# FFN weights rounded by quarters of the inner channels, part of them during block 0's FFN, with a shorter rounding and a two-operation norm end

## The chip, the core and the metric

The kernel runs on one core of a Trainium2 chip. The metric is the device time of one execution in microseconds. A core has engines that each work through a queue of their own in order: TensorE (PE in the profile; its weight loads are PEld), VectorE (DVE), ScalarE (ACT) and GpSimd (POOL). SyncE (SP) issues most of the DMAs. An instruction whose operands aren't ready holds up everything queued behind it on its engine. SBUF is the working memory of 128 partitions; PSUM holds what TensorE accumulates.

## The reference, cut to what matters

The input x has 4096 tokens (4 sequences of 1024) of 512 channels. Two residual parts follow each other; both begin and end with a layer norm (LN, without gain here unless named):

```
n   = LN(x)
q, v, g = n Wq^T, n Wv^T, silu(n Wg^T)
ret = scan over the tokens of a sequence: state = lambda * state + v
o   = ( LN(q * ret) * gamma + beta ) * g            # "attention's norm end"
x1  = x + LN(o Wo^T)

m    = LN(x1)
gate = silu( (m @ fp8(gate_w)) * gate_scale )       # 512 -> 1536 inner channels
up   =       (m @ fp8(up_w))   * up_scale
out  = x1 + LN( ((gate * up) @ fp8(down_w)) * down_scale )   # 1536 -> 512
```

`fp8(w)` rounds a float32 weight to float8 e4m3 and back to float32: three bits behind the leading one, a fixed step below 2^-6, and NaN for what is too large (the largest value is 448). It has to be done once for the three FFN matrices, 3 x 786,432 numbers, before they are used.

## The kernel before, in words

**Tiles and blocks.** The tokens are worked off in 8 blocks (`NB`) of 512 (`TB`), each in 4 groups (`NS`) of 128 tokens. Channels lie in `NC` = 4 chunks of 128, inner channels in `NI` = 12 chunks of 128.

**Attention** of a block is the generator `retention(t)` with `A_STEPS` = 17 steps. It norms and transposes x into `xnT`, projects (`project`, L191) onto v and q per chunk, scans (L228) and multiplies (L237) into `y`; takes the mean over channels with a matmul (`mu`, L241), subtracts it (L243), takes the variance the same way (L248 and L249) and forms `rstd` (L251 on ACT, L252 on DVE). Then per chunk c it projects onto g (L191, silu in L259) and finishes the norm on GpSimd: `y *= rstd` (L260), `y = y * gamma + lnb` (L261), `y *= g` (L265). Last, for each token group s, a matmul with Wo (L277), a norm of the result `o` (bn_stats L154 and L155, 1/sqrt on GpSimd in L159 and L160, scaling in L164), the residual sum on GpSimd (L284), a second norm giving `x1n`, and a transpose (L183) whose result is split into two float32r parts, `hi` by ACT (L184) and `lo` by DVE (L185), in the tile `x1nT`.

**FFN** of a block is `ffn(t)` with 13 steps. Step i projects onto gate and up for inner chunk i (`project_split`, L200, 8 matmuls each, since hi and lo both count), applies silu (L311), multiplies (L312), splits into `fuse` hi and lo (L314 on ACT, L315 on DVE), and issues the down projection of chunk i-1 (L301). The last step scales, norms, adds and stores the four groups (L323 to L326).

**Rounding** is the generator `round_weights()`: 12 pieces of 128 x 1536 numbers. Each piece gets a scratch tile `scr` (w and c side by side), a DMA of the weights into w (L136 or L138), and then seven DVE operations and one ACT operation (L139 to L148). Pieces 0 to 7 are rows of gate and up in turn (a chunk of 128 input channels, all 1536 inner ones), pieces 8 to 11 are down. So no inner chunk of gate is complete before the seventh piece.

**Buffers that count here.** `scr` and `x1nT` share the tag `"x1n"` of the pool `big`, which has two buffers: a piece that is being rounded takes one, and so does each block's `x1nT` from attention's Wo stage until the last matmul of that block's FFN. The pool `ps_a` of PSUM has two buffers (tag `"pa"`), used for all of attention's matmul results and transposes; `ps_f` has two for gate and up.

**Order.** The Python code emits work in an interleaved order, and the framework then lays out each engine's queue: work that was emitted earlier goes first, and an operation emitted later fills in where the earlier one isn't ready by the framework's own plan. At run time the queues are fixed. `together(main, main_steps, other, other_steps, after)` emits one step of `main`, then as many of `other` as keep it in proportion. Attention 0 is emitted with all 12 pieces; then FFN t with attention t+1; the last FFN alone. Tiles are tracked by region: the first down matmul of block 0 runs before the last piece of `down_sb` is written (174.98 us and 185.87 us in the trace).

Of the kernel before, what the change touches and what calls it, by code (L numbers as in the profile page):

```python
# [10 lines left out]
F32 = mybir.dt.float32  # L11
I32 = mybir.dt.int32
F32R = mybir.dt.float32r
AF = mybir.ActivationFunctionType
ALU = mybir.AluOpType

P = 128
# [5 lines left out]
def retention_ffn_sandwich(  # L23
# [19 lines left out]
    nc = tc.nc  # L43
    NT, D = x.shape
    I = gate_w.shape[1]
    NC = D // P
    NI = I // P
# [4 lines left out]
    const = ctx.enter_context(tc.tile_pool(name="const", bufs=1))  # L52
# [20 lines left out]
    def load_const(src, cols, name):  # L73
        t = const.tile([P, cols], F32, tag=name, name=name)
        nc.scalar.dma_start(t, src)
        return t
# [12 lines left out]
    gamma_sb = load_const(gamma, NC, "gamma_sb")  # L89
    lnb_sb = load_const(lnb, NC, "lnb_sb")  # L90
# [4 lines left out]
    gate_sb = wpool.tile([P, NC, I], F32R, tag="gate_sb", name="gate_sb")  # L95
    up_sb = wpool.tile([P, NC, I], F32R, tag="up_sb", name="up_sb")
    down_sb = wpool.tile([P, NI, D], F32R, tag="down_sb", name="down_sb")
    gate_v = gate_w.rearrange("(c p) f -> p c f", p=P)
    up_v = up_w.rearrange("(c p) f -> p c f", p=P)
    down_v = down_w.rearrange("(c p) f -> p c f", p=P)  # L100
    RC = NI // NC
    pieces = []
    for c in range(NC):
        pieces += [(gate_sb[:, c, :], gate_v[:, c, :]), (up_sb[:, c, :], up_v[:, c, :])]
    for c in range(NC):
        pieces.append((down_sb[:, RC * c : RC * c + RC, :], down_v[:, RC * c : RC * c + RC, :]))
    gs_sb = load_const(gate_s, NI, "gs_sb")
    us_sb = load_const(up_s, NI, "us_sb")
    ds_sb = load_const(down_s.to_broadcast([P, D]), D, "ds_sb")
# [5 lines left out]
    nc.vector.memset(mean_w, 1.0 / D)  # L115
    eps_sb = const.tile([P, 1], F32, tag="eps_sb", name="eps_sb")
    nc.vector.memset(eps_sb, EPS)
    nhalf = const.tile([P, NS], F32, tag="nhalf", name="nhalf")
    nc.vector.memset(nhalf, -0.5)
    carry = const.tile([P, NC], F32, tag="carry", name="carry")  # L120
# [7 lines left out]
    def round_weights():  # L128


        for n, (dst, src) in enumerate(pieces):
            scr = big.tile([P, 2, I], F32, tag="x1n", name=f"scr_{n}", bufs=2)
            w, c = scr[:, 0, :], scr[:, 1, :]
            if len(dst.shape) == 3:
                dst = dst.rearrange("p c f -> p (c f)")
                nc.sync.dma_start(w.rearrange("p (c f) -> p c f", f=D), src)  # L136
            else:
                nc.sync.dma_start(w, src)  # L138
            nc.vector.tensor_scalar(  # L139
                c.bitcast(I32), w.bitcast(I32), 0x7F800000, None, ALU.bitwise_and  # L140
            )
            nc.vector.tensor_scalar(c, c, 2.0**-6, 1.5 * 2.0**20, ALU.max, ALU.mult)
            nc.vector.tensor_tensor(w, w, c, ALU.add)
            nc.vector.tensor_tensor(w, w, c, ALU.subtract)
            nc.scalar.activation(c, w, AF.Square)
            nc.vector.tensor_scalar(c, c, 448.0**2, 448.0**2, ALU.max, ALU.subtract)
            nc.vector.tensor_scalar(c, c, 3.0e38, 0.0, ALU.mult, ALU.mult)
            nc.vector.tensor_tensor(dst, w, c, ALU.add)  # L148
            yield


    def stats(src, mv):
        st = small.tile([P, 6], F32, tag="st", name="st")
        nc.vector.bn_stats(st, src)  # L154
        nc.vector.bn_aggr(mv, st)  # L155
# [7 lines left out]
    def center_scale(dst, src, mean, rstd):  # L163
        nc.vector.tensor_scalar(dst, src, mean, rstd, ALU.subtract, ALU.mult)  # L164
# [41 lines left out]
    def retention(t, give):  # L206
        xt = xs[t]

        mv4 = small.tile([P, NS, 2], F32, tag="mv4", name="mv4")
        for s in range(NS):  # L210
            stats(xt[s], mv4[:, s, :])
        rstd4 = rstd_of(mv4[:, :, 1], NS)
        xnT = big.tile([P, NC, TB], F32, tag="xnT", name=f"xnT_{t}")
        for s in range(NS):
            xn = work.tile([P, D], F32, tag="tok", name=f"xn_{t}_{s}", bufs=5)
            center_scale(xn, xt[s], mv4[:, s, 0:1], rstd4[:, s : s + 1])
            to_channels(xnT, xn, s)
            if s % 2 == 1:
                yield


        y = big.tile([P, NC, TB], F32, tag="y", name=f"y_{t}")
        for c in range(NC):
            pv = project(ps_a, "pa", wv_sb, c, xnT)
            pq = project(ps_a, "pa", wq_sb, c, xnT)
            ret = work.tile([P, TB], F32, tag="ret", name=f"ret_{t}_{c}")
            first = (t * TB) % seq == 0
            nc.vector.tensor_tensor_scan(  # L228
                ret,
                lam[:, c : c + 1].to_broadcast([P, TB]),  # L230
                pv,
                0.0 if first else carry[:, c : c + 1],
                ALU.mult,
                ALU.add,
            )
            nc.vector.tensor_copy(carry[:, c : c + 1], ret[:, TB - 1 : TB])
            nc.vector.tensor_tensor(y[:, c, :], pq, ret, ALU.mult)  # L237
            yield
        mu = ps_a.tile([P, TB], F32, tag="pa", name=f"mu_{t}")
        for c in range(NC):  # L240
            nc.tensor.matmul(mu, mean_w, y[:, c, :], start=(c == 0), stop=(c == NC - 1))  # L241
        for c in range(NC):
            nc.vector.tensor_tensor(y[:, c, :], y[:, c, :], mu, ALU.subtract)  # L243
        yield
        var = ps_a.tile([P, TB], F32, tag="pa", name=f"var_{t}")
        for c in range(NC):
            sq = work.tile([P, TB], F32, tag="ret", name=f"sq_{t}_{c}")
            nc.scalar.activation(sq, y[:, c, :], AF.Square)  # L248
            nc.tensor.matmul(var, mean_w, sq, start=(c == 0), stop=(c == NC - 1))  # L249
        rstd = work.tile([P, TB], F32, tag="rstd", name=f"rstd_{t}", bufs=1)  # L250
        nc.scalar.activation(rstd, var, AF.Sqrt, bias=eps_sb)  # L251
        nc.vector.reciprocal(rstd, rstd)  # L252
        yield


        for c in range(NC):
            pg = project(ps_a, "pa", wg_sb, c, xnT)
            g = work.tile([P, TB], F32, tag="sg", name=f"g_{t}_{c}", bufs=3)
            nc.scalar.activation(g, pg, AF.Silu)  # L259
            nc.gpsimd.tensor_tensor(y[:, c, :], y[:, c, :], rstd, ALU.mult)  # L260
            nc.gpsimd.tensor_scalar(  # L261
                y[:, c, :], y[:, c, :], gamma_sb[:, c : c + 1], lnb_sb[:, c : c + 1],
                ALU.mult, ALU.add,
            )
            nc.gpsimd.tensor_tensor(y[:, c, :], y[:, c, :], g, ALU.mult)  # L265
            yield

        x1nT = big.tile([P, 2, NC, TB], F32R, tag="x1n", name=f"x1nT_{t}", bufs=2)  # L270
        hi, lo = x1nT[:, 0, :, :], x1nT[:, 1, :, :]
        give((hi, lo))
        before = None
        for s in range(NS):
            po = ps_a.tile([P, D], F32, tag="pa", name=f"po_{t}_{s}")
            for c in range(NC):
                nc.tensor.matmul(  # L277
                    po, y[:, c, ts(s, P)], wo_sb[:, c, :], start=(c == 0), stop=(c == NC - 1)
                )
            if before is not None:  # L280
                to_channels_split(hi, lo, before, s - 1)
            o = work.tile([P, D], F32, tag="tok", name=f"o_{t}_{s}", bufs=5)
            norm(o, po)
            nc.gpsimd.tensor_tensor(xt[s], xt[s], o, ALU.add)  # L284
            before = work.tile([P, D], F32, tag="tok", name=f"x1n_{t}_{s}", bufs=5)
            norm(before, xt[s])
            yield
        to_channels_split(hi, lo, before, NS - 1)
        yield
# [42 lines left out]
    A_STEPS = 2 + NC + 1 + 1 + NC + NS + 1  # L332
    given = {}

    def together(main, main_steps, other, other_steps, after=0):

        done = 0
        for k in range(main_steps):
            next(main)
            upto = -(-other_steps * (k + 1 - after) // (main_steps - 1 - after))  # L340
            while done < min(upto, other_steps):
                next(other)
                done += 1

    def start(t):
        return retention(t, lambda z: given.__setitem__(t, z))

    for s in range(NS):
        load_x(1, s)
    together(start(0), A_STEPS, round_weights(), len(pieces))  # L350
    for t in range(NB):
        if t + 1 < NB:
            together(ffn(t, given[t]), NI + 1, start(t + 1), A_STEPS, after=1)
        else:
            together(ffn(t, given[t]), NI + 1, None, 0)


# [42 lines left out]
```

## Time and profile before

The time is 1233.34 us (median of 3 runs, 1232.6 to 1235.83). The profiled execution has a span of 1229.2 us and a mean granted TensorE clock of 0.963.

| engine | busy us | share of the span |
|---|---|---|
| PE | 1087.4 | 88% |
| PEld | 678.0 | 55% |
| DVE | 569.6 | 46% |
| POOL | 294.0 | 24% |
| ACT | 245.2 | 20% |

| event in the trace | us from the span's start |
|---|---|
| first matmul of the projections (L191) | 16.00 |
| first rounding operation (L139) | 27.75 |
| end of the matmuls of `mu` (L241) | 52.30 |
| end of the reciprocal (L252) | 75.87 |
| end of the last norm-end operation on POOL (L265) | 98.56 |
| first gate matmul of FFN 0 (L200) | 166.14 |
| last rounding operation (L148) | 187.63 |
| first gate matmul of FFN 1 | 301.94 |
| first gate matmul of FFN 7 | 1144.98 |
| last matmul | 1213.29 |

From FFN 0 to FFN 7 there are seven periods in 978.8 us, that is 139.8 us each; the first of them is 135.8 us. A line of the page's groups reads: source line, engine, operation, output<-inputs, shapes, count, then busy time in us and the mean of one in ns, then the idle time of the engine just before these operations and who ended it.

### The profile page before, as it was taken

How to read it: one execution, taken by the hardware profiler on the slowest of the kernel's cores; microseconds unless marked ns; L12 is line 12 of the kernel's file. 1: busy time of each engine (PE TensorE's matmuls, PEld its weight loads, DVE VectorE, ACT ScalarE, POOL GpSimd, SP SyncE). 2: the span in 40 equal slices, each digit the busy share in tenths (PEclk: the TensorE clock that was granted, in tenths of full speed). 3: DMA queues.
4: the chain of work that ended last, by engine and by line, in shares of the span. 5: the costliest groups of instructions: out<-in, count | busy, mean ns of one | idle time of the engine just before them, and what ended most of it. 6: DMA issues, size and time to landing. Idle time of an engine off the chain costs nothing. (4 is left out here: it accounts for less than half of the span.)

```text
span 1229.2 us, 9606 instructions
## 1 busy us (share of the span) xinstructions
PE 1087.4 (88%) x3712; PEld 678.0 (55%) x3712; DVE 569.6 (46%) x865; ACT 245.2 (20%) x358; POOL 294.0 (24%) x374
## 2 busy tenths in 40 slices
PE   6673369999899979999899989999899989999994
PEld 3221155566466655665556655666556655665683
DVE  3986883326432473316523373315623363324523
ACT  1130130311113111311103111211203111131221
POOL 0054310233203240043303240043303241033302
PEclk9876689999999999999999999999999999999998
DMA  7120200000200020000200010000200000000000
GB/s 274 51 77 26 77 26 1 1 1 1 69 1 0 1 69 1 1 1 1 69 1 1 0 55 14 1 1 1 69 1 1 1 34 26 1 1 0 35 1 34
DMA packets 15054, 31.31 MB, mean 25 GB/s; under 512 B 2080, under 2 KB 2080, under 8 KB 15008
## 3 DMA queue, kind: packets, MB, share of 16 engines
q1 hardware_dynamic: 14144, 30.41, 7.2%
q8 instruction: 29, 0.48, 0.2%
q10 hardware_dynamic: 864, 0.28, 0.1%
q14 instruction: 17, 0.14, 0.0%
HBM read 22.30 MB, written 8.39 MB: 25 GB/s over the span
## 5 line engine op out<-in xcount | busy, mean ns | idle before, releaser
L200 PE MATMUL po_pf<-x1nT,gate_sb 128*128 128x512 f32 x768 | 218.4, 423 | 0.7 <-ACT x1nT L184 0.7
L200 PE MATMUL po_pf<-x1nT,up_sb 128*128 128x512 f32 x768 | 195.9, 393 | 11.9 <-DVE gate L312 11.9
L301 PE MATMUL pd<-down_sb,fuse 128*128 128x512 f32 x768 | 195.5, 394 | 10.0 <-DVE fuse L315 10.0
L200 PEld LDWEIGHTS po_pf<-x1nT,gate_sb 128*128 128x128 f32 x768 | 143.6, 189 | 56.1 <-issue 23.4
L312 DVE SCALAR_TENSOR_TENSOR gate<-po_pf,us_sb,gate 128x512 f32<-128x512 f32 x96 | 71.1, 740 | 213.8 <-PE po_pf L200 213.1
L301 PEld LDWEIGHTS pd<-down_sb,fuse 128*128 128x128 f32 x768 | 142.3, 188 | 46.1 <-DVE fuse L315 16.3
L200 PEld LDWEIGHTS po_pf<-x1nT,up_sb 128*128 128x128 f32 x768 | 143.6, 188 | 43.5 <-DVE gate L312 14.8
L260 POOL TENSOR_TENSOR y<-y,rstd 128x512 f32<-128x512 f32 x32 | 46.1, 1460 | 497.8 <-DVE rstd L252 497.8
L277 PE MATMUL po<-wo_sb,y 128*128 128x512 f32 x256 | 123.1, 626 | 17.8 <-POOL y L265 9.6
L311 ACT ACTIVATE gate<-po_pf,gs_sb 128x512 f32<-128x512 f32 x96 | 66.2, 689 | 303.7 <-PE po_pf L200 271.0
L191 PE MATMUL po_pa<-xnT,wq_sb 128*128 128x512 f32 x256 | 116.9, 600 | 2.1 <-DVE y L237 2.1
L191 PE MATMUL po_pa<-xnT,wv_sb 128*128 128x512 f32 x256 | 115.2, 593 | 1.5 <-DVE ret L228 0.8
L191 PE MATMUL po_pa<-xnT,wg_sb 128*128 128x512 f32 x256 | 114.5, 595 | 0.0
L314 ACT CAST fuse<-gate 128x512 fp32r<-128x512 f32 x96 | 59.9, 624 | 215.4 <-DVE gate L312 186.1
L277 PEld LDWEIGHTS po<-wo_sb,y 128*128 128x128 f32 x256 | 50.0, 199 | 77.1 <-issue 48.6
L315 DVE TENSOR_TENSOR fuse<-gate,fuse 128x512 fp32r<-128x512 f32 x96 | 70.5, 734 | 45.6 <-ACT fuse L314 45.6
L159 POOL TENSOR_SCALAR rstd<-mv 128x1 f32<-128x1 f32 (+1 forms) x104 | 28.6, 275 | 262.6 <-DVE mv L155 260.6
L191 PEld LDWEIGHTS po_pa<-xnT,wq_sb 128*128 128x128 f32 x256 | 49.1, 192 | 64.8 <-issue 61.6
L191 PEld LDWEIGHTS po_pa<-xnT,wv_sb 128*128 128x128 f32 x256 | 48.3, 189 | 54.6 <-issue 50.3
L191 PEld LDWEIGHTS po_pa<-xnT,wg_sb 128*128 128x128 f32 x256 | 48.8, 191 | 53.4 <-issue 51.3
L265 POOL TENSOR_TENSOR y<-y,g 128x512 f32<-128x512 f32 x32 | 40.6, 1278 | 100.8 <-ACT g L259 100.8
L183 PE MATMUL pt<-ident,x1n 128*128 128x128 f32 x128 | 21.3, 292 | 49.0 <-DVE x1n L164 32.8
(58 smaller groups left out, 892.0 us busy)
## 6 DMA issues: line engine op xcount, KB each, us to landing
x<-in_x SPq DMA_DIRECT2D x32, 256.0 KB, 2.7
out<-d SPq DMA_DIRECT2D x32, 256.0 KB, 2.0
scr<-in_gate_w SPq DMA_DIRECT2D x4, 768.0 KB, 4.4
scr<-in_up_w SPq DMA_DIRECT2D x4, 768.0 KB, 4.4
scr<-in_down_w SPq DMA_DIRECT2D x4, 768.0 KB, 4.5
wv_sb<-in_wvT SPq DMA_DIRECT2D x2, 512.0 KB, 6.4
wq_sb<-in_wqT SPq DMA_DIRECT2D x2, 512.0 KB, 8.1
wg_sb<-in_wgT SPq DMA_DIRECT2D x2, 512.0 KB, 9.3
```

Of the source, the lines that this page charges most:

```text
L159: nc.gpsimd.tensor_scalar(r, var, EPS, 1.0, ALU.add, ALU.mult)
L183: nc.tensor.transpose(pt[:, c, :], src[:, ts(c, P)], ident)
L191: nc.tensor.matmul(po, w[:, c, ts(col, P)], xT[:, c, :], start=(c == 0), stop=(c == NC - 1))
L200: nc.tensor.matmul(po, w[:, c, ts(col, P)], part[:, c, :], start=(c == 0 and part is hi), stop=(c == NC - 1 and part is lo),)
L260: nc.gpsimd.tensor_tensor(y[:, c, :], y[:, c, :], rstd, ALU.mult)
L265: nc.gpsimd.tensor_tensor(y[:, c, :], y[:, c, :], g, ALU.mult)
L277: nc.tensor.matmul(po, y[:, c, ts(s, P)], wo_sb[:, c, :], start=(c == 0), stop=(c == NC - 1))
L301: nc.tensor.matmul(pds[s], f[:, h, ts(s, P)], down_sb[:, i, :], start=(i == 0 and h == 0), stop=(i == NI - 1 and h == 1),)
L311: nc.scalar.activation(g, pg, AF.Silu, scale=gs_sb[:, i : i + 1])
L312: nc.vector.scalar_tensor_tensor(g, pu, us_sb[:, i : i + 1], g, ALU.mult, ALU.mult)
L314: nc.scalar.copy(f[:, 0, :], g)
L315: nc.vector.tensor_tensor(f[:, 1, :], g, f[:, 0, :], ALU.subtract)
```

## The change

1. **Quarters.** The pieces are cut the other way: for each quarter q of the inner channels (384 of them, three chunks) one piece of gate, one of up and one of down. A piece has 128 x 1536 numbers as before. After the first three pieces, FFN steps 0 to 2 have all their weights.
2. **Half of them later.** Six pieces (quarters 0 and 1) are emitted over attention 0's 17 steps, the other six (quarters 2 and 3) over the first nine steps of FFN 0, beside attention 1. `together` now takes any number of companions, each with its steps, a start and an end.
3. **Shorter rounding.** The lower bound on the exponent and the scaling move to ACT (a Relu with a bias and an Identity with scale and bias, the constants in two small tiles). What made a NaN of too large values with a Square and three DVE operations is now an ACT copy with a scale that overflows to infinity, and one DVE operation `c * 0 + w`, which also writes the result. A piece is then four DVE and three ACT operations.
4. **Norm end.** The three GpSimd operations per chunk become two DVE operations with two tensor inputs each: `(y * gamma) * rstd` and `(y + lnb) * g`.

It is for letting FFN 0 start with the first half of the weights, for taking work off VectorE while the weights are rounded, and for a shorter norm end.

```diff
-    RC = NI // NC
+    NQ = 4
+    IQ = I // NQ
     pieces = []
-    for c in range(NC):
-        pieces += [(gate_sb[:, c, :], gate_v[:, c, :]), (up_sb[:, c, :], up_v[:, c, :])]
-    for c in range(NC):
-        pieces.append((down_sb[:, RC * c : RC * c + RC, :], down_v[:, RC * c : RC * c + RC, :]))
+    for q in range(NQ):
+        pieces += [
+            (gate_sb[:, :, ts(q, IQ)], gate_v[:, :, ts(q, IQ)]),
+            (up_sb[:, :, ts(q, IQ)], up_v[:, :, ts(q, IQ)]),
+            (down_sb[:, ts(q, NI // NQ), :], down_v[:, ts(q, NI // NQ), :]),
+        ]
...
+            nc.sync.dma_start(as_dst(w), src)
             nc.vector.tensor_scalar(
                 c.bitcast(I32), w.bitcast(I32), 0x7F800000, None, ALU.bitwise_and
             )
-            nc.vector.tensor_scalar(c, c, 2.0**-6, 1.5 * 2.0**20, ALU.max, ALU.mult)
+            nc.scalar.activation(c, c, AF.Relu, bias=neg_low)
+            nc.scalar.activation(c, c, AF.Identity, scale=1.5 * 2.0**20, bias=low_unit)
             nc.vector.tensor_tensor(w, w, c, ALU.add)
             nc.vector.tensor_tensor(w, w, c, ALU.subtract)
-            nc.scalar.activation(c, w, AF.Square)
-            nc.vector.tensor_scalar(c, c, 448.0**2, 448.0**2, ALU.max, ALU.subtract)
-            nc.vector.tensor_scalar(c, c, 3.0e38, 0.0, ALU.mult, ALU.mult)
-            nc.vector.tensor_tensor(dst, w, c, ALU.add)
+            nc.scalar.activation(c, w, AF.Copy, scale=1.1 * 2.0**119)
+            nc.vector.scalar_tensor_tensor(dst, as_dst(c), 0.0, as_dst(w), ALU.mult, ALU.add)
             yield
...
-            nc.gpsimd.tensor_tensor(y[:, c, :], y[:, c, :], rstd, ALU.mult)
-            nc.gpsimd.tensor_scalar(
-                y[:, c, :], y[:, c, :], gamma_sb[:, c : c + 1], lnb_sb[:, c : c + 1],
-                ALU.mult, ALU.add,
+            nc.vector.scalar_tensor_tensor(
+                y[:, c, :], y[:, c, :], gamma_sb[:, c : c + 1], rstd, ALU.mult, ALU.mult
             )
-            nc.gpsimd.tensor_tensor(y[:, c, :], y[:, c, :], g, ALU.mult)
+            nc.vector.scalar_tensor_tensor(
+                y[:, c, :], y[:, c, :], lnb_sb[:, c : c + 1], g, ALU.add, ALU.mult
+            )
...
-    together(start(0), A_STEPS, round_weights(), len(pieces))
+    rounding = round_weights()
+    FIRST = 6
+    together(start(0), A_STEPS, (rounding, FIRST, 0, A_STEPS))
     for t in range(NB):
+        others = []
+        if t == 0:
+            others.append((rounding, len(pieces) - FIRST, 0, NI - 3))
         if t + 1 < NB:
-            together(ffn(t, given[t]), NI + 1, start(t + 1), A_STEPS, after=1)
-        else:
-            together(ffn(t, given[t]), NI + 1, None, 0)
+            others.append((start(t + 1), A_STEPS, 1, NI))
+        together(ffn(t, given[t]), NI + 1, *others)
```

More of the change, by code (lines that the diff above doesn't have):

```diff
@@ L117, in retention_ffn_sandwich @@
     nc.vector.memset(eps_sb, EPS)
+    neg_low = const.tile([P, 1], F32, tag="neg_low", name="neg_low")
+    nc.vector.memset(neg_low, -(2.0**-6))
+    low_unit = const.tile([P, 1], F32, tag="low_unit", name="low_unit")
+    nc.vector.memset(low_unit, 1.5 * 2.0**14)
     nhalf = const.tile([P, NS], F32, tag="nhalf", name="nhalf")
@@ L133, in round_weights, with as_dst @@
             w, c = scr[:, 0, :], scr[:, 1, :]
-            if len(dst.shape) == 3:
-                dst = dst.rearrange("p c f -> p (c f)")
-                nc.sync.dma_start(w.rearrange("p (c f) -> p c f", f=D), src)
-            else:
-                nc.sync.dma_start(w, src)
+            def as_dst(z):
+                return z.rearrange("p (a b) -> p a b", a=dst.shape[1])
+            nc.sync.dma_start(as_dst(w), src)
             nc.vector.tensor_scalar(
@@ L333, in retention_ffn_sandwich, with together @@
     given = {}
-    def together(main, main_steps, other, other_steps, after=0):
-        done = 0
+    def together(main, main_steps, *others):
+        done = [0] * len(others)
         for k in range(main_steps):
             next(main)
[L340 to L343, printed above, removed]
+            for j, (other, steps, after, by) in enumerate(others):
+                upto = -(-steps * (k + 1 - after) // (by - after))
+                while done[j] < min(upto, steps):
+                    next(other)
+                    done[j] += 1
     def start(t):
@@ L349, in retention_ffn_sandwich @@
         load_x(1, s)
-    together(start(0), A_STEPS, round_weights(), len(pieces))
+    rounding = round_weights()
+    FIRST = 6
+    together(start(0), A_STEPS, (rounding, FIRST, 0, A_STEPS))
     for t in range(NB):
+        others = []
+        if t == 0:
+            others.append((rounding, len(pieces) - FIRST, 0, NI - 3))
         if t + 1 < NB:
-            together(ffn(t, given[t]), NI + 1, start(t + 1), A_STEPS, after=1)
-        else:
-            together(ffn(t, given[t]), NI + 1, None, 0)
+            others.append((start(t + 1), A_STEPS, 1, NI))
+        together(ffn(t, given[t]), NI + 1, *others)
 def kernel(**inputs):
```

## The prediction, made before the changed kernel ran

> **What bounds the kernel now.** I read the page's 40 slices first (one slice is 30.7 us), to see which stages have different limits.
>
> ```profile
> PE   6673369999899979999899989999899989999994
> DVE  3986883326432473316523373315623363324523
> PEclk9876689999999999999999999999999999999998
> ```
>
> From slice 7 on PE is nearly full and DVE is far from it: TensorE sets the pace of seven of the eight periods. In the first six slices it is the other way round, and the clock granted to PE is lowest there. So I cut the first stages out with the view of stretches, whose columns are the stretch, its length, busy us (and counts) of PE, PEld, DVE, ACT and POOL, the clock, the DMA share and GB/s. The cuts are the events of the table above: start of the projections, end of mu, end of the reciprocal, end of the norm end, start of FFN 0, start of FFN 1.
>
> ```profile
> 16.00:52.30 36.30, 33.40 (x72) 14.02 (x72) 27.69 (x29) 2.97 (x2) 0.00 (x0) 0.95 0.41 152
> 52.30:75.90 23.60, 13.56 (x22) 5.24 (x23) 23.41 (x21) 9.19 (x10) 0.00 (x0) 0.71 0.20 67
> 75.90:98.60 22.70, 13.14 (x25) 4.77 (x24) 13.81 (x9) 4.54 (x5) 22.62 (x12) 0.83 0.11 35
> 98.60:166.10 67.50, 20.86 (x43) 9.29 (x42) 57.31 (x66) 9.78 (x9) 19.79 (x20) 0.65 0.14 47
> 166.10:301.90 135.80, 133.72 (x464) 84.86 (x464) 61.06 (x89) 29.59 (x44) 26.08 (x34) 0.99 0.02 6
> ```
>
> Attention 0 ends at 166 us. The same attention costs PE about 66 us when it runs dense inside a later block (eight v and q projections at 3.43, mu 3.4, var 3.7, four wg and four Wo groups at 3.43 each, transposes 4). DVE holds the difference: it is busy 23.4 of 23.6 us before the reciprocal and 57.3 of 67.5 in the Wo stage, and the same view restricted to `scr` gives rounding 20.7, 18.2, 13.8 and 43.8 us of the four stretches: 96.5 of DVE's 122.2 busy us. Only between 75.9 and 98.6 is POOL the full engine: the norm end. How this reaches PE is told by PE's own waits up to 230 us (total, times, longest):
>
> ```profile
> PE pt L183 <- DVE x1n L164: 21.5, 2, 11.3
> PE pt L183 <- DVE x1nT L185: 16.2, 1, 16.2
> PE po L277 <- POOL y L265: 9.6, 2, 6.2
> PE po L277 <- DVE o L164: 8.3, 2, 7.9
> ```
>
> and DVE's timeline shows one such wait being made (start, length):
>
> ```profile
> 109.55 0.67 DVE L154 BATCH_NORM_STATS2 st<-po 128x6 f32<-128x512 f32 x1
> 110.13 1.74 DVE L143 TENSOR_TENSOR scr<-scr 128x1536 f32<-128x1536 f32 x1
> ...
> 119.85 0.96 DVE L147 TENSOR_SCALAR scr<-scr 128x1536 f32<-128x1536 f32 x1
> 120.72 0.18 DVE L155 BATCH_NORM_AGGREGATE mv<-st 128x2 f32<-128x6 f32 x1
> ```
>
> The 0.18 us that finish a statistic come 10.5 us after it, behind rounding, while PE waits for the norm. In block 0's later part the same chain, from the first statistic of a group to x1n, takes 6.5 us (268.88 to 275.36). So: first 166 us DVE-bound by rounding, then PE-bound.
>
> **Prices.** The answer for the tile `scr` (ns, min/median/max):
>
> ```profile
> L139 DVE TENSOR_SCALAR scr<-scr x12: 935/956/2028, 27.7 to 174.7; 128x1536 int32<-128x1536 int32 x12
> L143 DVE TENSOR_TENSOR scr<-scr x12: 1742/1753/1760, 29.7 to 177.7; 128x1536 f32<-128x1536 f32 x12
> L145 ACT ACTIVATE scr<-scr x12: 1477/1486/1487, 34.0 to 181.5; 128x1536 f32<-128x1536 f32 x12
> DMA to landing us min/median/max: 4.1/4.5/9.1
> ```
>
> **What the Trainium skill says.** (1) "VectorE: DVE Perf Modes", in the perf-mode tier table: float32 in SBUF runs at double rate with one tensor input, at single rate with two. The trace agrees: 956 against 1753 ns above. The new `scalar_tensor_tensor` isn't in that table; it has two tensor inputs, so I price it like tensor_tensor: 1.75 us at 1536, and 0.75 at 512 by L312, which is the same operation with one input in PSUM. Bounds 0.65 (the fastest L312) and 0.80. (2) "ScalarE: Activation LUTs", Table sets: cheap functions such as relu, copy and identity are in every set. So no table load for the new ones; the trace has Square (L145) and the casts without a load of their own, and shows loads before L251, L311, L124 and L259 only (17, at 1.28 us). (3) Same page, What ACT_TABLE_LOAD costs: a per-partition bias adds about 93 ns; so Relu and Identity are 1.58 each by L145's 1.49 plus that (an estimate; no 1536-wide row shows it), the copy 1.49. (4) "GPSIMD Engine Reference", Specifications: GpSimd shares its SBUF interfaces with VectorE. The trace agrees: the first two L260 and L261 take 4.59 and 8.46 us in pairs beside rounding, where the medians of one are 1.29 and 0.77.
>
> **The change part by part.**
>
> *Shorter rounding.* DVE per piece before: 4 x 0.96 + 3 x 1.75 = 9.1 us. After: 0.96 + 3 x 1.75 = 6.2. ACT goes from 1.49 to 4.65; ACT was busy 26 of 150 us in attention 0, so this lies beside other work, though its 1.5 us pieces can hold up a silu or copy behind them.
>
> *Fewer pieces in attention 0.* Before, 96.5 us of rounding on DVE; after, 6 x 6.2 = 37. The norm end adds 8 x 0.75 = 6. Net on DVE: -53.5. Two ways to the new start of FFN 0. By DVE's budget: DVE was busy 122 of 150 us (81%), its gaps being mostly waits that the other work makes; taking 53 us out of a full queue gives 166 - 53 = 113. By the chain: projections end with mu at about 51, as before (now 52.3; two pieces still share that stage); subtraction, variance and reciprocal take 10 us undisturbed, 14 with one or two rounding operations ahead of a hop, giving 65; wg runs on PE meanwhile until about 79 at worst, and the norm end on DVE is 6 us, half of it before g; then the Wo stage. Undisturbed that is 30 us: two Wo groups, then the third group's matmul waits for the first group's o and transposes (two PSUM buffers), the fourth for the second's, and the last group's chain of 6.5 plus transpose, hi and lo closes it. With two pieces (12.4 us of DVE) among its hops I take 36. From a Wo start between 73 and 79: 109 to 115. I take 113, so **-53**.
>
> *Half the rounding in FFN 0.* DVE in FFN 0's period had 61 us in 135.8, 12 of them rounding; it becomes 61 - 12 + 37 + 6 = 92, or 68%. ACT becomes about 56. Both fit, but two waits appear. First, queueing: in a step without attention matmuls, L312 has some 2.6 us before PE needs its PSUM buffer (down and gate matmuls of 1.81 each, less its own 0.75 and latencies), so one 1.75 us operation ahead of it is hidden and two are not. PE showed such stops already (7 for L312, 13 for L315, 22 us in all, at block changes). I take +4. Second, and new: `x1nT` of block 0 holds one of the two "x1n" buffers until FFN 0 ends, so the six pieces follow each other through the other one. A piece then costs DMA 4.5, DVE 6.2, ACT 4.65 and some seven handovers of 0.1: 16 us at least. DVE's 68% load makes it perhaps 19. With piece 6 started 5 us before FFN 0, the pieces are ready at 14, 33, 52, 71, 90 and 109 us after FFN 0's start. They are wanted (FFN steps 6 and 9 and the down projection of 9, by the times of before) at 69, 69, 81, 102, 104 and 116; all in time. But block 1's `x1nT` needs the same buffer for L184 at 111.5, and behind that write stand the transpose's PSUM buffer, the next Wo matmul and, in PE's queue, the whole FFN. It just fits; I take +3 for the cases where it doesn't.
>
> *Smaller DMA runs.* Gate and up now come in runs of 1.5 KB instead of 6 KB. Down already came in runs of 2 KB and landed in 4.5 us against 4.4: nothing.
>
> *Norm end in blocks 1 to 7.* POOL loses 118 us in all (46.1 + 31.3 + 40.6), DVE gains 64 x 0.75 = 48, 6 per period of 140 that had 58 busy. PE waits for L265 only twice in the whole kernel, both in attention 0; later the wg groups lie between FFN steps and hide it. The DVE operations fall where DVE is idle 7 to 10 us before L312. Nothing, with bounds of -3 and +5 over seven periods.
>
> **Sum:** 1233.3 - 53 + 4 + 3 = **1187**.
>
> **Rivals.** *The clean case (0.15):* the planned order keeps rounding out of the Wo chain (FFN 0 at 105) and FFN 0 hides its half: 1233 - 61 = 1172. For it: 66 us of PE work and a chain of about 102; against: the queues of before weren't so laid. *The single buffer is the new bound (0.15):* in the full queue of before a piece held its buffer 20 to 35 us (43.4 to 64.3; 68.9 to 104.5). At 25 us in FFN 0 the sixth is done at 145 against 111.5: +34 instead of +7, so 1214. A framework that took the interleaved quarters for overlapping regions (contiguous ones it tells apart) would make the second up projection wait for piece 7 and cost about as much. *Slower (0.06):* pieces at 32 us, as in the worst of before, are done at 187: 1233 - 53 + 76 = 1256. Against it: DVE at 68% instead of full. *No gain (0.02):* FFN 0 starts early and gives exactly that back.
>
> **How the numbers follow.** My forecast has 0.62. The range must hold 0.8: from a little below the clean case, 1168, to 1212, which takes in the forecast with +-12 for where the hops fall, the norm end's bounds, and the milder half of the single-buffer case. Faster comes from the first three cases, 0.92; within 0.3% 0.02; slower 0.06.
>
> **What would show it.** First gate matmul of FFN 0 at 105 to 118 us (right) or beyond 130 (the DVE budget is wrong). DVE per piece 6.2 us, no table load beside Relu. No PE wait for L265's successor. In FFN 0, a period of 136 to 146; a long PE wait for x1nT's lo or for a weight piece there, with DMA issues of `scr` spaced 25 us or more, would mean the buffer. Periods 2 to 7 unchanged at about 140; if they move by more than 1 us each, my zero for the norm end is the error.

## The result, and the profile after

The changed kernel takes **1189.8 us** (median of 4 runs, 1188.13 to 1191.93) against 1233.33 (1232.6 to 1235.83): a ratio of 0.9645, 95% interval 0.9624 to 0.9665. The profiled execution has a span of 1188.0 us. First the slices of its page (29.7 us each):

```profile
PE   5684999989999899998999989998899979999994
DVE  3876667564344733456242652436433473335523
PEclk9897899999999999999999999999999999999998
```

PE is full from slice 5 on instead of slice 7. The first slices are still ragged, but DVE shows mostly sixes and sevens there, where before it showed mostly eights and nines. The view of stretches, cut at the same events as before (start of the projections, end of mu, end of the reciprocal, end of the norm end, start of FFN 0, start of FFN 1; the columns are those of the prediction):

```profile
16.00:54.90 38.90, 33.94 (x72) 14.21 (x72) 24.97 (x25) 15.70 (x11) 0.00 (x0) 0.91 0.37 134
54.90:74.20 19.30, 13.89 (x27) 5.90 (x28) 16.68 (x13) 13.93 (x14) 0.00 (x0) 0.82 0.12 42
74.20:81.40 7.20, 7.20 (x18) 3.23 (x17) 6.95 (x10) 1.20 (x2) 0.00 (x0) 1.00 0.35 109
81.40:118.90 37.50, 18.58 (x45) 8.11 (x43) 22.27 (x40) 6.88 (x7) 12.53 (x21) 0.76 0.08 21
118.90:259.70 140.80, 135.36 (x465) 85.44 (x465) 89.47 (x108) 54.77 (x61) 12.34 (x21) 0.98 0.09 29
```

| stretch | before, us | after, us | difference |
|---|---|---|---|
| projections to the end of mu | 36.3 | 38.9 | +2.6 |
| to the end of the reciprocal | 23.6 | 19.3 | -4.3 |
| norm end | 22.7 | 7.2 | -15.5 |
| Wo stage, to the start of FFN 0 | 67.5 | 37.5 | -30.0 |
| FFN 0 to FFN 1 | 135.8 | 140.8 | +5.0 |
| FFN 1 to FFN 7 | 843.0 | 844.1 | +1.1 |
| FFN 7 to the end | 84.2 | 84.2 | 0 |

The differences sum to -41.1 us; the two spans differ by 41.2, the medians by 43.5. All of the gain lies ahead of FFN 0, which starts 47.2 us sooner. Of these 47.2 us, 39.9 are waits of PE (29.3 us from the projections on, instead of 69.2) and 7.3 are busy time of PE for the same work (73.6 instead of 81.0), at a mean granted clock of 0.85 instead of 0.76. Whether the clock follows from the shorter waits was not tested.

Of PE's waits up to 119 us (total, times, longest; left out are small ones, and one of 11.4 us ahead of the projections, which was 11.6 before):

```profile
PE pt L192 <- DVE x1n L173: 15.7, 3, 9.2
PE po_pa L200 <- DVE ret L237: 4.8, 1, 4.8
PE var L258 <- ACT sq L257: 4.5, 1, 4.5
```

The wait for POOL's norm end (9.6 us) and the long one for the lo part of x1nT (16.2 us) are gone. The wait of a transpose for x1n (L192 is the old L183, L173 the old L164) stays, shorter, and the one of the variance for its squares fell from 10.0 to 4.5.

### The profile page after: what moved, and what is told of

Read it like the earlier page. It is cut to its first block, busy times and chain, and to the rows that moved or that the text cites. A ratio compares the mean times of both kernels' runs of the same rounds, so it can differ in the third digit from the quotient of the medians.

```text
span 1188.0 us, 9580 instructions
## 1 busy us (share of the span) xinstructions
PE 1084.3 (91%) x3712; PEld 679.4 (57%) x3712; DVE 579.7 (49%) x895; ACT 281.4 (24%) x382; POOL 168.8 (14%) x278
## 5 line engine op out<-in xcount | busy, mean ns | idle before, releaser
L168 POOL TENSOR_SCALAR rstd<-mv 128x1 f32<-128x1 f32 (+1 forms) x104 | 24.2, 232 | 953.4 <-DVE mv L164 951.4
L321 DVE SCALAR_TENSOR_TENSOR gate<-po_pf,us_sb,gate 128x512 f32<-128x512 f32 x96 | 71.1, 740 | 123.0 <-PE po_pf L209 122.0
L200 PE MATMUL po_pa<-xnT,wv_sb 128*128 128x512 f32 x256 | 117.6, 603 | 5.5 <-DVE ret L237 4.8
L286 PE MATMUL po<-wo_sb,y 128*128 128x512 f32 x256 | 118.2, 606 | 2.6 <-DVE x1nT L194 1.4
L163 DVE BATCH_NORM_STATS2 st<-x 128x6 f32<-128x512 f32 x64 | 42.9, 681 | 42.5 <-POOL x L293 37.7
L169 POOL TENSOR_TENSOR rstd<-rstd,nhalf 128x1 f32<-128x1 f32 (+1 forms) x104 | 60.2, 579 | 8.7
L272 DVE SCALAR_TENSOR_TENSOR y<-y,lnb_sb,g 128x512 f32<-128x512 f32 x32 | 23.9, 750 | 74.0 <-ACT g L268 74.0
```

The source lines that it names most:

```text
L168: nc.gpsimd.tensor_scalar(r, var, EPS, 1.0, ALU.add, ALU.mult)
L169: nc.gpsimd.tensor_tensor(r, r, nhalf[:, :n], ALU.pow)
L200: nc.tensor.matmul(po, w[:, c, ts(col, P)], xT[:, c, :], start=(c == 0), stop=(c == NC - 1))
L272: nc.vector.scalar_tensor_tensor(y[:, c, :], y[:, c, :], lnb_sb[:, c : c + 1], g, ALU.add, ALU.mult)
L286: nc.tensor.matmul(po, y[:, c, ts(s, P)], wo_sb[:, c, :], start=(c == 0), stop=(c == NC - 1))
L321: nc.vector.scalar_tensor_tensor(g, pu, us_sb[:, i : i + 1], g, ALU.mult, ALU.mult)
```

## The experiments

All times are medians, each taken beside runs of the kernel before on the same chip. The medians of the kernel before went from 1232.1 to 1234.4 us between these sets, so a difference of some 2 us between two rows is not shown by the times. "FFN 0 at" is the start of its first gate matmul in the profiled execution; the period runs from there to FFN 1's.

| kernel | time, us | ratio to before, 95% | FFN 0 at | period |
|---|---|---|---|---|
| before | 1233.3 | 1 | 166.1 | 135.8 |
| changed | 1189.8 | 0.9645 (0.9624 to 0.9665) | 118.9 | 140.8 |
| changed, norm end on POOL | 1197.4 | 0.9715 (0.9692 to 0.9738) | 128.5 | 140.6 |
| changed, old rounding | 1192.4 | 0.9669 (0.9646 to 0.9692) | 124.0 | 139.0 |
| changed, all pieces in attention 0 | 1215.6 | 0.9860 (0.9837 to 0.9883) | 147.9 | 137.4 |
| changed, pieces only copied | 1170.0 | 0.9490 (0.9462 to 0.9517) | 103.7 | 136.3 |
| before, shorter rounding | 1218.9 | 0.9878 (0.9853 to 0.9903) | 150.0 | 137.0 |
| before, norm end on DVE | 1228.4 | 0.9961 (0.9941 to 0.9981) | 162.7 | 136.1 |
| quarters and split alone | 1206.0 | 0.9773 (0.9745 to 0.9801) | 134.5 | 144.6 |
| changed, three pieces first | 1189.1 | 0.9641 (0.9610 to 0.9672) | 108.5 | 150.9 |
| changed, four pieces first | 1187.3 | 0.9623 (0.9601 to 0.9645) | 112.4 | 145.1 |
| pairs of smaller pieces | 1174.0 | 0.9519 (0.9498 to 0.9541) | 106.4 | 138.9 |
| smaller pieces, one at a time | 1192.0 | 0.9656 (0.9640 to 0.9672) | 104.3 | 155.9 |
| pairs, old rounding | 1181.8 | 0.9574 (0.9552 to 0.9595) | 111.7 | 140.7 |

In every one of them FFN 1 to FFN 7 takes 841.3 to 845.1 us, with no order by what was changed: within these 4 us, nothing in this change reaches the later blocks.

### Undoing one part at a time

**The norm end back on POOL.**

```diff
-            nc.vector.scalar_tensor_tensor(y[:, c, :], y[:, c, :], gamma_sb[:, c : c + 1], rstd, ALU.mult, ALU.mult)
-            nc.vector.scalar_tensor_tensor(y[:, c, :], y[:, c, :], lnb_sb[:, c : c + 1], g, ALU.add, ALU.mult)
+            nc.gpsimd.tensor_tensor(y[:, c, :], y[:, c, :], rstd, ALU.mult)
+            nc.gpsimd.tensor_scalar(y[:, c, :], y[:, c, :], gamma_sb[:, c : c + 1], lnb_sb[:, c : c + 1], ALU.mult, ALU.add)
+            nc.gpsimd.tensor_tensor(y[:, c, :], y[:, c, :], g, ALU.mult)
```

> The changed kernel with the norm end back on GpSimd (three operations per chunk), all else as changed. Theory 1 (the gain lies in attention 0, DVE's queue and the chain set it): the norm end between reciprocal and first Wo matmul was 22.7 us on POOL and is 7.2 on DVE; without heavy rounding beside it POOL needs about 4 x (1.29 + 0.77 + 1.28) = 13.4 us, so FFN 0 starts 6 to 15 us later (125 to 134) and the time is 1196 to 1204; periods from FFN 1 on stay at 140.2 to 141.7. Theory 2 (taking the norm end off POOL helps in every block): each of the seven later periods grows by 1.5 us or more, time above 1205. Theory 3 (the norm end is hidden by the wg matmuls): within 3 us of 1190.

Measured 1197.4, FFN 0 at 128.5, FFN 1 to FFN 7 in 844.4 us. Theory 1 holds; theory 2, a gain in every block, is refuted. POOL needed 14.2 us (76.5 to 90.7), where it needed 22.6 in the kernel before and DVE needs 7.2. So of the 15.5 us that the norm end got shorter, about half comes from the engine, the rest from what else changed. In the same view of PE's waits, up to 128 us, the old wait is back (L274 is the last norm-end operation):

```profile
PE po L286 <- POOL y L274: 5.0, 2, 4.0
```

It is smaller than the 9.6 of before. The trace fits less rounding beside POOL as the reason: the first two `y * gamma + lnb` took 8.46 us in the kernel before, with rounding on DVE all through them, and 1.52 here, where DVE's last rounding operation ahead of them had ended at 78.0 and they began at 80.3.

**The old rounding.**

```diff
-            nc.scalar.activation(c, c, AF.Relu, bias=neg_low)
-            nc.scalar.activation(c, c, AF.Identity, scale=1.5 * 2.0**20, bias=low_unit)
+            nc.vector.tensor_scalar(c, c, 2.0**-6, 1.5 * 2.0**20, ALU.max, ALU.mult)
             nc.vector.tensor_tensor(w, w, c, ALU.add)
             nc.vector.tensor_tensor(w, w, c, ALU.subtract)
-            nc.scalar.activation(c, w, AF.Copy, scale=1.1 * 2.0**119)
-            nc.vector.scalar_tensor_tensor(dst, as_dst(c), 0.0, as_dst(w), ALU.mult, ALU.add)
+            nc.scalar.activation(c, w, AF.Square)
+            nc.vector.tensor_scalar(c, c, 448.0**2, 448.0**2, ALU.max, ALU.subtract)
+            nc.vector.tensor_scalar(c, c, 3.0e38, 0.0, ALU.mult, ALU.mult)
+            nc.vector.tensor_tensor(dst, as_dst(w), as_dst(c), ALU.add)
```

> The changed kernel with the old rounding sequence (seven DVE operations and one ACT operation per piece), quarters, the split and the norm end as changed. Theory 1 (DVE's budget in attention 0): DVE carries 6 x 2.9 = 17 us more before FFN 0 and as much within it; FFN 0 starts 12 to 17 us later (131 to 136), its period grows by 2 to 6 us with DVE near 107 of 143 us: 1203 to 1213. Rival (only the place of the work counts; the shorter rounding trades DVE time for ACT waits of 1.6 us in a row): within 5 us of 1190, FFN 0 at 119 to 123.

Measured 1192.4: only 2.6 us more, with intervals that overlap, where theory 1 said 13 to 23. The rival's time holds; FFN 0's start, 124.0, is 1 us beyond the rival's range and 7 short of theory 1's. The stretch from the projections to FFN 0, of the changed kernel and then of this one:

```profile
16.00:118.94 102.94, 73.61 (x160) 31.44 (x160) 70.88 (x84) 37.70 (x33) 12.53 (x21) 0.85 0.22 74
16.00:124.03 108.03, 74.07 (x160) 31.69 (x161) 85.91 (x101) 19.43 (x22) 17.20 (x20) 0.87 0.22 74
```

DVE has 15.0 us more to do and the stretch is 5.1 longer; the rest comes out of DVE's idle time, 32.1 us in the first line and 22.1 in the second. So the shorter sequence mostly made DVE idle. The price per us of DVE that I had taken, close to 1, is 0.34 here.

**All pieces in attention 0.**

```diff
-    FIRST = 6
+    FIRST = 12
```

> The changed kernel with all 12 pieces emitted during attention 0, nothing left for FFN 0; rounding and norm end as changed. Theory 1 (DVE's budget): 37 us of rounding return to DVE before FFN 0, at 0.8 to 1.0 us of delay each, so FFN 0 starts at 148 to 156, its period falls from 140.8 to about 136: 1215 to 1222. Rival (DVE has slack in attention 0 once the sequence is short, PE and the chain of norms set the start): FFN 0 at 119 to 128, time 1185 to 1195. The share of the split in the gain is read from this.

Measured 1215.6, FFN 0 at 147.9: in theory 1's range for the time (and 0.1 us short of it for the start). Emitting six pieces later is worth 29 us of start, for 3.3 us of FFN 0's period. Not all six had been in the way: in this run 11 pieces ended before FFN 0 began and the twelfth after, in the changed kernel six, so it is 5.8 us for each of five. This is the largest part of the change.

**The pieces only copied** (the rounding is left out).

```diff
-            nc.vector.tensor_scalar(c.bitcast(I32), w.bitcast(I32), 0x7F800000, None, ALU.bitwise_and)
...
+            nc.scalar.copy(dst, as_dst(w))
```

> The rounding itself is left out: each piece is loaded and copied by one ACT operation, with no DVE work; the rest as changed. This bounds what rounding can cost at all. Theory 1: attention 0 is then its bare chain, FFN 0 starts at 100 to 104, its period is 135 to 137: 1167 to 1172, so that the changed kernel has some 20 us left to give. Rival (PE, the loads and the clock already set attention 0): FFN 0 at 112 to 119 and a time above 1180.

Measured 1170.0, FFN 0 at 103.7, period 136.3: without rounding, attention 0 takes what I had put together from the undisturbed hops (102). Its parts don't fit as well: the first Wo matmul came at 68.4 (72, by 102 less the 30 of the Wo stage) and the Wo stage took 35.3 instead of 30, two errors that nearly cancel. What rounding still costs in the changed kernel, over loading and copying, is 19.8 us.

### One part at a time on the kernel before

**Shorter rounding alone** (row pieces; the rounding lines as in the change).

> The kernel before with the shorter rounding alone (row pieces, all 12 in attention 0, norm end on GpSimd). In the changed kernel the shorter rounding was worth 2.6 us although it takes 35 us off DVE in all. Theory A (DVE time is worth something only where DVE's queue is full): before, DVE was busy 122 of 150 us in attention 0, so here the same 35 us give 18 to 30: FFN 0 at 136 to 148, time 1203 to 1215. Theory B (the shorter form trades DVE time for ACT waits and is worth little anywhere): within 6 us of 1233.

Measured 1218.9, a gain of 14.3: between the two theories, below A's 18. DVE had 26 us less to do before FFN 0 (96.0 busy from 16 to 150.0, against 122.3 up to 166.1), and FFN 0 came 16.1 sooner: 0.6 us per us, more than in the changed kernel, still not 1.

**Norm end on DVE alone** (the two new operations in the kernel before).

> The kernel before with the norm end on DVE alone. Undoing it in the changed kernel cost 7.6 us. Theory A (it shortens the stage between reciprocal and first Wo matmul, 22.7 us on POOL): but DVE did 13.8 us of rounding in that stage, which must go elsewhere in a full queue, so 5 to 12 us: 1221 to 1228, FFN 0 at 154 to 161. Rival (the whole stage is saved): 15 us or more, 1218 or less. Rival (DVE was full, so the 6 us added to it cost what is saved): within 3 us of 1233.

Measured 1228.4, a gain of 4.8, just short of theory A's 5 to 12, with FFN 0 at 162.7 (154 to 161 expected). The Wo matmuls began at 88.9 instead of 90.3, and PE then waited 9.9 us for the norm end on DVE, whose operations stood among the rounding. The norm end on DVE gave 4.8 us alone and 7.6 on top of the others, where DVE has less rounding to do; the two figures are too close for the times alone to tell them apart.

**Quarters and split alone** (old rounding, norm end on POOL).

> Quarters and the split alone: six pieces in attention 0 and six in FFN 0, with the old rounding and the norm end on GpSimd. Undoing the split in the changed kernel cost 25.8 us, undoing the two others 7.6 and 2.6. Theory A (the three parts relieve the same full queue, so each is worth more alone than on top of the others): 30 to 38 us, time 1195 to 1203, FFN 0 at 128 to 136. Theory B (the parts add up): 25 to 27 us, 1206 to 1208.

Measured 1206.0, a gain of 27.2 us, at the edge of B's range. In the profiled execution FFN 0 starts 31.7 us sooner, and its period, 144.6, gives 8.8 of it back. The old rounding in FFN 0 isn't the reason by itself: with the norm end on DVE the same six pieces leave a period of 139.0. Against that run PE waits 3.2 us more, of which 3.1 is one wait for the norm end on POOL (L275), and is busy 2.4 us more at a clock of 0.96 instead of 0.98. With the shorter rounding the norm end on POOL made no such wait (period 140.6), so in these traces it takes both. The split is worth 27 alone and 26 on top of the others. The three gains alone add up to 46.3 us against 43.5 together, but that isn't additivity: rounding is worth 14.3 alone and 2.6 last, the norm end 4.8 alone and 7.6 last.

### Where FFN 0's share ends

**Three pieces first, nine in FFN 0.**

```diff
-    FIRST = 6
+    FIRST = 3
```

> The changed kernel with three pieces emitted over attention 0 and nine over the first nine steps of FFN 0, one per step. Theory (the one free buffer of the tag shared by scratch and x1nT is what limits FFN 0): pieces took 16 to 21 us each through it, so nine end at 145 us or more after FFN 0's start, while step 3 wants the fourth and fifth at 33 and block 1's x1nT wants the buffer at 115; FFN 0 starts at 106 to 114, but its period is 165 to 190: 1205 to 1235. Rival (the buffer is no limit and DVE has room in FFN 0): FFN 0 at 106 to 114 and a period of 141 to 148: 1178 to 1190, better than the changed kernel.

Measured 1189.1: FFN 0 at 108.5 as both said, a period of 150.9, between the two; the time lies within the rival's 1178 to 1190. The last two pieces were late (PE waited 0.5 us for the one, 3.8 for the other). Of the waits of PE from 100 to 265 us, and DVE's timeline of the last piece (L157 is its last operation):

```profile
PE pd L310 <- DVE down_sb L157: 3.8, 1, 3.8
```
```profile
241.53 1.76 DVE L157 SCALAR_TENSOR_TENSOR down_sb<-scr 128x1536 fp32r<-128x1536 f32 x1
```

It ends 134.8 us after FFN 0's start. With six pieces left for FFN 0 the last one ended 99.7 after it and PE waited for none. The late pieces are 4.3 of the 10.1 us by which the period is longer than the changed kernel's; 3.6 are other waits, and 2.3 are busy time of PE, at a clock of 0.96 instead of 0.98.

**Four pieces first** (FIRST = 4).

> The changed kernel with four pieces over attention 0 and eight over FFN 0's first nine steps. With three pieces FFN 0 began at 108.5 and its period was 150.9 (last piece done 135 us after its start, one wait of 3.8 us for it); with six, 118.9 and 140.8 (last piece done after 100). Theory (attention 0 pays some 3.5 us a piece, FFN 0 pays only once the last piece comes later than about 111 to 116 us): last piece at about 120, FFN 0 at 111 to 113, period 143 to 146, time 1185 to 1189. Rival (FFN 0 pays as much per piece as attention 0 does, so that the split point doesn't matter between three and six): 1189 to 1190.

Measured 1187.3, FFN 0 at 112.4, period 145.1, last piece 117.3 us after the start. The numbers are the theory's, but so near 1189.8 that the times don't tell it from the rival, and the trace has none of the waits for a late piece that the theory speaks of: of the 4.4 us by which the period is longer, 1.5 are scattered waits and 2.9 busy time of PE, at a clock of 0.96 instead of 0.98. What attention 0 gives back, FFN 0 takes: FFN 1 starts at 259.3, 257.6 and 259.7 us for three, four and six pieces.

**Pairs: two smaller pieces side by side in one buffer.** A buffer of the shared tag has 16 KB per partition, because x1nT needs it; a piece of 1536 used 12. With sixths of the inner channels a piece has 1024 numbers and two fit.

```diff
-    NQ = 4
+    NQ = 6
...
-        for n, (dst, src) in enumerate(pieces):
-            scr = big.tile([P, 2, I], F32, tag="x1n", name=f"scr_{n}", bufs=2)
-            w, c = scr[:, 0, :], scr[:, 1, :]
+        for n in range(0, len(pieces), 2):
+            scr = big.tile([P, 2, 2, W], F32, tag="x1n", name=f"scr_{n}", bufs=2)
+            for h, (dst, src) in enumerate(pieces[n : n + 2]):
+                w, c = scr[:, h, 0, :], scr[:, h, 1, :]
...
-    FIRST = 6
+    FIRST = 3
...
-            others.append((rounding, len(pieces) - FIRST, 0, NI - 3))
+            others.append((rounding, len(pieces) // 2 - FIRST, 0, NI - 4))
```

> The changed kernel with 18 pieces of 1024 numbers (sixths of the inner channels), two of them side by side in one buffer of the shared tag, so that the second's load and DVE work fill the first's waits; three pairs over attention 0 (as many numbers as four pieces), six pairs over FFN 0's first eight steps. Theory (one piece after the other through the free buffer is what stretches FFN 0 when more is moved there): a pair of 2048 numbers takes 16 to 18 us instead of 17 for 1536, so the last is done 100 to 108 us after FFN 0's start, in time; FFN 0 at 109 to 114, period 140 to 142, time 1181 to 1186. Rival (DVE's load in FFN 0 stretches it, not the buffer; smaller operations only add overhead): period 145 or more, 1188 or more.

Measured **1174.0** (1169.77 to 1174.96): better than both kernels, and better than the theory's range; FFN 0 at 106.4 (I said 109 to 114) and a period of 138.9. It emits as many numbers before FFN 0 as the kernel with four pieces and does the same operations. Its stretch of FFN 0 (from 2.4 us ahead of it), and the end of its last piece:

```profile
104.00:245.00 141.00, 136.44 (x468) 86.04 (x466) 97.98 (x132) 60.60 (x75) 12.52 (x22) 0.97 0.11 38
```
```profile
195.67 1.22 DVE L158 SCALAR_TENSOR_TENSOR down_sb<-scr 128x1024 fp32r<-128x1024 f32 x1
```

The last piece is done 90.5 us after FFN 0's start. In the period itself DVE carries 95.6 us against 89.5 in the changed kernel, and the period is shorter: DVE's load isn't what stretches FFN 0.

**The same small pieces, one at a time.**

```diff
-        for n in range(0, len(pieces), 2):
+        for n in range(len(pieces)):
...
-            for h, (dst, src) in enumerate(pieces[n : n + 2]):
+            for h, (dst, src) in enumerate(pieces[n : n + 1]):
...
-    FIRST = 3
+    FIRST = 6
...
-            others.append((rounding, len(pieces) // 2 - FIRST, 0, NI - 4))
+            others.append((rounding, len(pieces) - FIRST, 0, NI - 4))
```

> The kernel with 18 pieces of 1024 numbers, but each alone in its buffer; six over attention 0, twelve over FFN 0's first eight steps. The kernel with two of them side by side gave 1174.0 (FFN 0 at 106.4, period 138.9). It differs from this one only in what is in flight at once. Theory (two in one buffer keep FFN 0 short; the smaller operations shorten attention 0's hops): FFN 0 at 104 to 110 as with pairs, but the pieces follow each other at 12.5 to 14 us, the last done 150 us or more after FFN 0's start, period 152 to 170: 1187 to 1205. Rival (the smaller operation alone made the gain, in both stages): period 139 to 143, 1173 to 1180.

Measured 1192.0: FFN 0 at 104.3, period 155.9, the last piece ending 146 us after FFN 0's start (expected 150 or more). As the theory had it: the smaller pieces give attention 0 its early end (104.3 and 106.4, against 112.4 for the same numbers emitted in pieces of 1536), and two in flight keep FFN 0 at 138.9 instead of 155.9. The rival is refuted. Part of the early end is that less was done: before FFN 0 six and seven pieces of 1024 ended here, and five of 1536 there. At the same numbers done, six of 1024 against the four of 1536 with three pieces first, it is 104.3 against 108.5. In FFN 0 PE waits 13.6 us more than with pairs and is busy 3.4 more, but only 1.7 us is a wait for a piece by itself; how the rest comes of late pieces was not followed.

**Pairs with the old rounding** (the diff of the old rounding above, at 1024 numbers).

> The kernel with pairs of pieces of 1024 numbers, with the old rounding sequence (seven DVE operations and one ACT operation, against four and three). In the changed kernel the shorter sequence was worth 2.6 us. Theory (DVE isn't full, neither in attention 0 nor in FFN 0; what counts is how many operations get ahead of a hop of the chain, and how long a piece holds its buffer): within 2 to 6 us of 1174, that is 1176 to 1180. Rival (with the waits gone DVE is the limit, and its 17 us before FFN 0 and 17 in it now count): 1190 or more.

Measured 1181.8, 7.8 us above pairs (6.8 by the two ratios): between theory and rival. FFN 0 began 5.3 us later and its period was 1.8 longer. The shorter sequence seems to count for more where the other waits are gone, but nowhere near the DVE time it saves: DVE was busy 9.9 us more before FFN 0 and 21.2 more in its period, 116.8 of 140.7 us.

## Why the prediction was right, and where its steps were off

The forecast was 1187, the measurement 1189.8. By its steps:

- **The first 166 us are the place, seven periods are not.** Right: -47.2 us ahead of FFN 0, +6.0 in all after it. FFN 1 to FFN 7 took 844.1 us with the norm end on DVE and 844.4 with it back on POOL, so its zero for the later blocks stands, as far as the 4 us between the kernels tell.
- **Prices.** DVE per piece 0.95 + 1.76 + 1.75 + 1.76 = 6.2, as said; the new norm-end operations 0.744 and 0.750; Relu and Identity 1.576 and 1.575 (estimate 1.58), with the table loads still 17. The trace now shows what the Trainium skill gave for the bias ("ScalarE: Activation LUTs", What ACT_TABLE_LOAD costs, about 93 ns): 94 ns, by 1.576 less 1.482 for the copy. Landing took 4.6 and 4.7 us in runs of 1.5 KB against 4.4 in runs of 6 KB.
- **DVE in FFN 0** 89.5 us (92 said), ACT 54.8 (56 said). The pieces ended 15.6, 31.7, 47.9, 64.7, 83.6 and 99.7 us after FFN 0's start (14, 33, 52, 71, 90 and 109 said), all in time. The period grew by 5.0 instead of 7, which is near by luck: neither of the two waits behind the 7 came. From 119 to 260 us PE has no wait for L321 (the old L312), on which I had put 4, and no new one for x1nT or a piece, on which I had put 3. Instead PE waits 1.4 us for block 1's mu and 1.5 for its variance, all in all 5.4 instead of 2.0, and is busy 135.4 us instead of 133.8, at a clock of 0.98 instead of 0.99.
- **The step that was mis-sized: -53 for FFN 0's start, which measured -47.2.** The chain was put too short in front: mu at 51 said, 54.9 measured (PE waits 4.8 us there for a scan, L237, that stands behind four rounding operations), reciprocal done at 65 said, 74.2 measured, and the Wo stage 39.1 us from its first matmul instead of 36. The rounding lay further forward than I had it: DVE did 17.5, 11.2, 1.6 and 6.2 us of it in the four stretches, so nearly three pieces ahead of mu where I had two, and one in the Wo stage where I had two. And the undisturbed Wo stage, 30 us in my sum, takes 35.3 with the rounding left out. Only the wg matmuls, which hide the reciprocal, kept it together: the Wo start was 79.8, just past the end of my range.
- **The step that was wrong though it agreed: DVE's budget.** I took 53 us "out of a full queue" and got 113, close to the chain's answer. The runs show no such rate. Per us of DVE time removed before FFN 0, its start moved by 0.34 us (shorter rounding in the changed kernel), 0.6 (in the kernel before) and 0.96 (whole pieces moved away: 101.1 to 70.9 busy, 28.9 us). For the whole change it is 0.92 (122.3 to 70.9 busy, 47.2 us), near 1 because moving pieces is the largest part of it. What moves with a whole piece, and not with a shorter one, is its number of operations that can stand ahead of a hop, its ACT work and its hold on a buffer. Which of these three makes the difference of 0.34 and 0.96 was not separated.
- **A wait in the kernel before that I had not taken apart.** Of the waits of before, "x1nT L185, 16.2" looks like rounding ahead of L185 on DVE. Lines of before's timelines, DVE's and ACT's:

```profile
143.00 1.75 DVE L148 TENSOR_TENSOR down_sb<-scr 128x1536 fp32r<-128x1536 f32 x1
```
```profile
143.17 1.49 ACT L145 ACTIVATE scr<-scr 128x1536 f32<-128x1536 f32 x1 [5.45 <-DVE scr L144]
144.86 0.59 ACT L184 CAST x1nT<-pt 128x512 fp32r<-128x512 f32 x1 [0.21 <-DVE down_sb L148]
```

The transpose had been done since 117; the cast began 0.11 us after the last operation of a piece of down, with which it shares nothing but the tag of their buffer. So the cast waited for a buffer. But it also stood in ACT's queue behind L145 of the next piece, itself released by rounding on DVE, and that ended at 144.66. With this order in ACT's queue the buffer alone cost 0.2 us. Whether the framework put the cast so far back because of the buffer is open. This is read from the trace only; no run takes the wait away.

Of the rivals, the single buffer shows with three pieces first and with small pieces one at a time, where pieces come late; not with four or six, where PE waits for none. The clean case is about what pairs reach (FFN 0 at 106.4, 1174.0).

## What to carry to other kernels

When one-time preparation delays the first useful work, moving part of it beside that work can pay more than making it shorter: here 26 us against 3 when one is undone in the changed kernel, 27 against 14 when one is done alone. Don't price a part by the busy time it takes off a busy engine; put the chain together from undisturbed hops, and take only what stands ahead of them. Smaller pieces next to a chain of short hops, and two of them in flight per buffer, were worth 16 us more for 4 us more of work on DVE.

## What the runs showed of the hardware that was not expected

The price of smaller operations is low: at 1024 numbers tensor_tensor took 1.22 us and the exponent mask 0.685, at 1536 1.75 and 0.95, so 18 small pieces cost DVE 78 us (18 x 4.34) against 12 x 6.2 = 74. And POOL is more easily disturbed than its median tells: of 32 `y * gamma + lnb` in the kernel before, two took 3.836 and 4.632 us, both with rounding operations on DVE all through them; the median is 0.766, and no other is over 0.777. DVE was disturbed as well: the exponent mask that ran beside POOL's first norm-end operations took 2.03 us, where its median is 0.956.
